# A recommendation kernel on Trainium2: history rows transposed into PSUM instead of through TensorE, and some rows fetched by SyncE

## The chip, the cores and the metric

The kernel runs on one core of a Trainium2 chip. The metric is the time of one execution on the device in microseconds; the median of three runs stands for a kernel. The core's engines are named as the profile names them: PE (TensorE, matrix products; PEld is its weight loading), DVE (VectorE), ACT (ScalarE), POOL (GpSimd) and SP (SyncE, which here only starts DMA transfers). PSUM is the memory into which PE writes; DVE and ACT can read and write it too. SBUF is the main memory on the core.

## The reference

A deep interest network for B = 16384 users with a history of L = 200 items each. Tables have D = 64 columns in float32, users and items 100000 rows.

```python
u, it, c = u_emb[user], i_emb[item], c_emb[cate]
h = i_emb[hist]                              # (200, 16384, 64)
itb = jnp.broadcast_to(it[None], h.shape)
feat = jnp.concatenate([h, itb, h - itb, h * itb], axis=-1)
a = dice(feat @ au_W1 + au_b1, au_alpha, axis=1)   # axis 1: over the users
w = a @ au_W2 + au_b2
cur = jnp.sum(w * h, axis=0)
z = jnp.concatenate([u, it, c, cur], axis=-1)
z = dice(z @ W1 + b1, alpha1, axis=0)
z = dice(z @ W2 + b2, alpha2, axis=0)
return z @ W3 + b3

def dice(x, alpha, axis):
    p = sigmoid((x - mean(x, axis)) * rsqrt(var(x, axis) + 1e-8))
    return x * (p + alpha * (1 - p))
```

Nearly all work is `h = i_emb[hist]`: 3.3 million rows of 256 bytes, each gathered from a random place, and the small attention layer on each. The mean and variance in `dice` go over all users of one history position, so no row of a position can be weighed before all its rows have been through the layer.

## The kernel before

The 16384 users are cut into 8 tiles of 2048 (128 partitions x 16 rows of 64). A step k handles tile c = k % 8 of history position l = k // 8; there are K = 1600 steps, in one list written out by hand (`step`), which each engine runs through in order. The engines are coupled by semaphores alone. In step k different things are done for different steps:

- SP starts `load_items(k + 1)` (L312): 512 KB of the transposed candidate items into one of four `itT` buffers. When c is 4 it also loads the indices of position l + 2 (L115).
- POOL does `fetch(k)`: 16 indirect gathers (L107), each 128 rows of 256 bytes, into one of 16 `rows` tiles.
- ACT does `gate(k - 10)` (L276): the sigmoid out of `xs` into PSUM buffer `pg`.
- `turn(k - 1)`: DVE transposes `rows` in 32x32 blocks into `hT` in SBUF, four instructions (L126); PE multiplies `hT` by the identity `same` into PSUM buffer `py` (through `layer`, L131), so that DVE can read the turned rows there.
- DVE adds the item's part (`hidden(k - 3)`, L300) and takes statistics (`measure(k - 3)`, two `bn_stats`, L305). When k - 3 is the last tile of a position, the norm follows: 28 small DVE instructions (L322 to L340, and the root in L142 to L148), and only then the gate.
- `product(k - 1)`: PE multiplies `hT` by `blk_h` into `px`; DVE forms `hm = py * itT` (L316); PE adds `hm` times `blk_m`.
- `weights(k - 10)` and `weigh(k - 10)` on DVE: L279 to L285 make the weights, L295 multiplies `rows` by them, L297 adds to `cur`.

A gather of step k may overwrite its `rows` tile when L295 of step k - 16, done in step k - 6, is through. So POOL can be up to six steps ahead of DVE, not more. Matrix products of float32 appear as two instructions each, so `layer` with one weight is four matmuls and four weight loads on PE.

Ahead of the loop the items are gathered and turned, the categories are looked up and the weights are laid out; after it come 128 gathers of user rows and the two upper layers.

Of the kernel before, what the change touches and what calls it, by code (L numbers as in the profile page):

```python
# [14 lines left out]
P = 128  # L15
D = 64
# [8 lines left out]
ITEMS = 4  # L25
IDX = 3


@with_exitstack
def din_kernel(  # L30
# [41 lines left out]
    def make(name, *shape, dt=F32):  # L72
        return const.tile(list(shape), dt, name=name)
# [18 lines left out]
    cur = [make(f"cur{c}", P, CD) for c in range(ND)]  # L92
    hm = make("hm", P, CD)
    total = py[:, :S]
    part = make("part", P, S)
    w = pg[:, :TD]
# [3 lines left out]
    ids = [idx[(i - 1) % IDX if i == 0 else (L + i - 1) % IDX] for i in range(2)]  # L100
    stats = [make(f"st{i}", P, 2 * ND, STATS) for i in range(3)]
    cate_ids = make("cate_ids", P, TD, dt=I32)
# [46 lines left out]

    same = make("same", P, P)  # L150
    blk_h = make("blk_h", P, P)
# [107 lines left out]
    def head_numbers():  # L259
# [3 lines left out]
        for t, n in ((same_a, ZA), (same_b, ZB)):  # L263
            nc.vector.tensor_single_scalar(lane, lanes, n - 1, ALU.bitwise_and)
            nc.vector.tensor_copy(t, lane)
            nc.vector.tensor_scalar(t, t, 0.0, n / P, ALU.is_equal, ALU.mult)

    def fetch(k):
# [9 lines left out]
    def weights(k):  # L278
        nc.vector.scalar_tensor_tensor(py, pg, au_1al, xs[k % XR], ALU.mult, ALU.mult)  # L279
        nc.vector.transpose(pg, py)  # L280
        nc.vector.reduce_sum(total, pg.rearrange("p (n a) -> p n a", a=S), axis=mybir.AxisListType.X)  # L281
        nc.vector.tensor_copy(part[P // 2 :], total[P // 2 :])  # L282
        for i in range(2):
            for g in range(2):
                nc.vector.scalar_tensor_tensor(  # L285
                    w[quarter(i, g)],
                    total[quarter(0, g), ts(i, TD)], au_bias2[quarter(0, g)], part[quarter(1, g), ts(i, TD)],
                    ALU.add, ALU.add,
                )

    def weigh(k):
        of = py.rearrange("p (n d) -> p n d", d=D)
        if k < ND:
            of = cur[k].rearrange("p (n d) -> p n d", d=D)
        nc.vector.tensor_mul(of, rows[k % ROWS], w.unsqueeze(2).to_broadcast([P, TD, D]))  # L295
        if k >= ND:
            nc.vector.tensor_add(cur[k % ND], py, cur[k % ND])  # L297

# [8 lines left out]
    def turn(k):  # L307
        transpose(hT[k % TURNED], rows[k % ROWS])
        layer(py, [(same, hT[k % TURNED])])

    def load_items(k):
        nc.sync.dma_start(itT[k % ITEMS], items[k % ND])  # L312

    def product(k):
        layer(px[k % 2], [(blk_h, hT[k % TURNED])], last=False)
        nc.vector.tensor_mul(hm, py, itT[k % ITEMS])  # L316
        layer(px[k % 2], [(blk_m, hm)], first=False)

# [25 lines left out]
    def step(k):  # L344

        def has(j):
            return 0 <= j < K

        if has(k + 1):
            load_items(k + 1)  # L350
        if has(k):
            l, c = divmod(k, ND)
            if c == 4 and l + 2 < L:
                load_hist_ids((l + 2) % IDX, l + 2)
            if c == 4 and l + 2 == L:
                load_ids(ids[1], r_user)
            fetch(k)
# [12 lines left out]
        if has(k - 1):  # L370
            product(k - 1)
        if has(k - LAG):
            weights(k - LAG)
            weigh(k - LAG)

    NK = -(-c_emb.shape[0] // P)
# [8 lines left out]
    def category_numbers():  # L385
# [22 lines left out]
        nc.vector.tensor_copy(of_row, rank)  # L408
        nc.vector.tensor_single_scalar(same, lanes, float(P), ALU.is_equal)

    def category(c, i):
# [17 lines left out]
        nc.scalar.copy(xs[c % XR][:, ts(i, CH)], to)  # L429

    with tc.manual_schedule():
        load_ids(ids[0], r_item)
        for l in range(min(2, L)):
            load_hist_ids(l, l)
        nc.sync.dma_start(cate_ids, r_cate.rearrange("(p n) -> p n", n=NT)[:, (ND - 1) * TD :])
        nc.gpsimd.iota(lanes, pattern=[[1, P]], base=P, channel_multiplier=-1)
# [3 lines left out]
        attention_weights()  # L440
        extra_unit()
        head_weights()

        halves_of = [(c, i) for c in range(ND - 1) for i in range(2)]
        for c in range(ND + 1):
# [13 lines left out]
            if c < ND:  # L459
                category(*halves_of.pop(0))  # L460
        load_items(0)
        head_numbers()
        for half in halves_of:
            category(*half)
        transpose(xs[ND - 1], rows[ND])
        for c in range(ND):
            nc.sync.dma_start(cates[c], xs[c % XR])

    za = [xs[(K - XR + c) % XR] for c in range(ND)]
# [183 lines left out]
```

## Time and profile before

| | |
|---|---|
| median of the runs | 38346.77 us |
| the runs | 38344.67, 38346.77, 38373.36 us |
| profiled execution | 38084.07 us |
| its span, first to last instruction | 38082.3 us |
| granted PE clock, mean | 0.646 |
| busy: PE / PEld | 14569.6 us (38%) / 5252.9 us (14%) |
| busy: DVE | 23384.9 us (61%) |
| busy: ACT | 2000.3 us (5%) |
| busy: POOL | 24410.9 us (64%) |
| DMA | 45 GB/s over the span |

The loop takes 98% of the span (its first product starts at 501.6 us, its last at 37813.6), and all its 40 slices on the page look alike, so one history position stands for the whole. No engine is busy for more than two thirds of the time. A row of a timeline gives start, duration, engine, line, operation and, in brackets, how long the engine had been idle and what ended it; "issue" is a wait for nothing that the profile shows, and "remote" one that something outside the record ended.

### The profile page before, as it was taken

Reading aid. Unit: us, or ns where it says so; the run is one execution under the profiler, and the core shown is the slowest. Engines: PE = TensorE matmul, PEld = TensorE weight load, DVE = VectorE, ACT = ScalarE, POOL = GpSimd, SP = SyncE. Lnnn points to the kernel's source line nnn. Section 1 sums busy time; section 2 is a strip of 40 time slices with the busy share of each in tenths; the row PEclk is TensorE's granted clock in tenths of the full one; section 3 lists DMA queues with packets and bytes.
Section 4 is the critical chain, followed back from the end, with each engine's and each line's share of the span. In section 5 each row is a group of like instructions: output and inputs, shape, how many; then the busy total and the mean of one; then the engine's idle time right before and its main releaser. Section 6 shows DMA issues by size and latency. Waiting matters only on the chain.

```text
span 38082.3 us, 118503 instructions
## 1 busy us (share of the span) xinstructions
PE 14569.6 (38%) x20100; PEld 5252.9 (14%) x20100; DVE 23384.9 (61%) x34932; ACT 2000.3 (5%) x1667; POOL 24410.9 (64%) x25879
## 2 busy tenths in 40 slices
PE   4333333333333333333333333333333333333334
PEld 1111111111111111111111111111111111111111
DVE  4666666666666666666666666666666666666666
ACT  0000000000000000000000000000000000000001
POOL 5666666666666666666666666666666666666665
PEclk7666666666666666666666666666666666666666
DMA  1111111111111111111111111111111111111111
GB/s 45 45 45 45 45 46 45 46 46 46 46 45 46 45 46 45 46 45 46 46 46 45 46 45 46 45 45 46 45 46 46 46 46 45 45 45 45 45 46 42
DMA packets 1103495, 1727.07 MB, mean 45 GB/s; under 512 B 454022, under 2 KB 479878, under 8 KB 1102726
## 3 DMA queue, kind: packets, MB, share of 16 engines
q0 software_dynamic: 827904, 849.43, 9.9%
q1 hardware_dynamic: 274246, 869.99, 6.7%
q14 instruction: 612, 5.01, 0.0%
q8 instruction: 157, 2.57, 0.0%
q10 hardware_dynamic: 576, 0.07, 0.0%
HBM read 1709.19 MB, written 8.52 MB: 45 GB/s over the span
## 4 chain that ended last, share of the span: by engine, by line
DVE 52%; another core or an unknown queue 26%; issue 14%; POOL 6%; DMA 1%; PE 1%; DVEq 1%; ACT 0%; POOLq 0%; ACTq 0%
DVE hT L126 10%; POOL rows L107 6%; DVE py L279 5%; DVE pg L280 5%; DVE hm L316 5%; DVE py L281 5%; DVE xs L300 4%; DVE py L295 4%; DVE pg L285 4%; DVE st L305 3%; DVE rs L148 1%; DVE t L147 1%; DVE t L146 1%; DMA rows<-in_L_rec_i_emb,idx 1%
## 5 line engine op out<-in xcount | busy, mean ns | idle before, releaser
L107 POOL DMA_INDIRECT rows<-in_L_rec_i_emb,idx x25728 | 24274.4, 944 | 13406.8 <-issue 7402.7
L131 PE MATMUL py<-hT,same 128*128 128x512 f32 x6400 | 6032.2, 1091 | 9968.1 <-DVE hT L126 5063.1
L131 PE MATMUL px<-hm,blk_m 128*128 128x512 f32 x6400 | 4506.7, 843 | 13260.1 <-DVE hm L316 7045.1
L316 DVE TENSOR_TENSOR hm<-py,itT 128x1024 f32<-128x1024 f32 x1600 | 1945.9, 1216 | 10239.3 <-remote 8060.6
L126 DVE STREAM_TRANSPOSE hT<-rows 64x512 f32<-64x512 f32 x6400 | 4499.9, 703 | 416.8 <-issue 327.6
L131 PE MATMUL px<-hT,blk_h 128*128 128x512 f32 x6400 | 3979.0, 755 | 1.0 <-issue 0.5
L276 ACT ACTIVATE pg<-xs,sh,rs 128x1024 f32<-128x1024 f32 x1600 | 1932.5, 1208 | 35232.2 <-DVE py L295 23733.1
L131 PEld LDWEIGHTS px<-hm,blk_m 128*128 128x128 f32 x6400 | 1530.6, 257 | 15673.8 <-DVE hm L316 7533.2
L131 PEld LDWEIGHTS py<-hT,same 128*128 128x128 f32 x6400 | 1771.9, 311 | 13673.5 <-DVE hT L126 7103.9
L279 DVE SCALAR_TENSOR_TENSOR py<-pg,au_1al,xs 128x1024 f32<-128x1024 f32 x1600 | 2068.3, 1293 | 540.1 <-remote 213.3
L131 PEld LDWEIGHTS px<-hT,blk_h 128*128 128x128 f32 x6400 | 1787.4, 282 | 2881.9 <-issue 2339.1
L280 DVE STREAM_TRANSPOSE pg<-py 128x1024 f32<-128x1024 f32 x1600 | 2024.5, 1265 | 172.3 <-DVE py L279 122.2
L305 DVE BATCH_NORM_STATS2 st<-xs 128x6 f32<-128x512 f32 x3200 | 2058.4, 685 | 55.0
L300 DVE TENSOR_TENSOR xs<-px,itp 128x1024 f32<-128x1024 f32 x1600 | 1959.7, 1225 | 130.0 <-issue 83.4
L281 DVE TENSOR_REDUCE py<-pg 128x32 f32<-128x1024 f32 x1600 | 1972.7, 1233 | 72.5 <-DVE pg L280 0.8
L295 DVE TENSOR_TENSOR py<-rows,pg 128x1024 f32<-128x1024 f32 x1592 | 1957.3, 1229 | 55.3 <-issue 0.7
L297 DVE TENSOR_TENSOR cur<-py,cur 128x1024 f32<-128x1024 f32 x1592 | 1948.5, 1224 | 56.3 <-issue 0.9
L285 DVE SCALAR_TENSOR_TENSOR pg<-py,au_bias,part 32x16 f32<-32x16 f32 x6400 | 1530.6, 239 | 227.6 <-issue 1.2
L147 DVE SCALAR_TENSOR_TENSOR t<-t,v 128x1 f32<-128x1 f32 x808 | 131.0, 162 | 608.2 <-DVE t L146 268.1
L148 DVE SCALAR_TENSOR_TENSOR rs<-t,rs 128x1 f32<-128x1 f32 x800 | 129.2, 161 | 605.5 <-DVE t L147 396.5
L146 DVE TENSOR_TENSOR t<-rs 128x1 f32<-128x1 f32 x800 | 127.8, 160 | 468.6 <-DVE rs L148 262.0
L282 DVE COPY part<-py 64x32 f32<-64x32 f32 x1600 | 311.2, 195 | 88.0 <-DVE py L281 32.0
(158 smaller groups left out, 1835.2 us busy)
## 6 DMA issues: line engine op xcount, KB each, us to landing
itT<-items SPq DMA_DIRECT2D x1608, 512.0 KB
rows<-in_L_rec_i_emb,idx POOLq DMA_INDIRECT x25728
idx<-in_r_hist SPq DMA_DIRECT2D x200, 64.0 KB
items<-itT SPq DMA_DIRECT2D x8, 512.0 KB
cates<-xs SPq DMA_DIRECT2D x8, 512.0 KB
itp<-cates SPq DMA_DIRECT2D x8, 512.0 KB
rows<-in_L_rec_u_emb,idx POOLq DMA_INDIRECT x128
cur<-in_L_rec_c_emb SPq DMA_DIRECT2D x14, 32.0 KB
```

Of the source, the lines that this page charges most:

```text
L107: nc.gpsimd.indirect_dma_start(out=dst[:, n, :], out_offset=None, in_=table, in_offset=bass.IndirectOffsetOnAxis(ap=ids, axis=0),)
L126: nc.vector.transpose(by_tile(dst[ts(e, D)], i)[:, n0:n1], of[ts(i, D), n0:n1, ts(e, S)])
L131: nc.tensor.matmul(dst[:, ts(i, CH)], lhsT, rhs[:, ts(i, CH)], start=(first and j == 0), stop=(last and j == len(pairs) - 1), skip_group_c ...
L279: nc.vector.scalar_tensor_tensor(py, pg, au_1al, xs[k % XR], ALU.mult, ALU.mult)
L280: nc.vector.transpose(pg, py)
L281: nc.vector.reduce_sum(total, pg.rearrange("p (n a) -> p n a", a=S), axis=mybir.AxisListType.X)
L285: nc.vector.scalar_tensor_tensor(w[quarter(i, g)], total[quarter(0, g), ts(i, TD)], au_bias2[quarter(0, g)], part[quarter(1, g), ts(i, TD) ...
L295: nc.vector.tensor_mul(of, rows[k % ROWS], w.unsqueeze(2).to_broadcast([P, TD, D]))
L297: nc.vector.tensor_add(cur[k % ND], py, cur[k % ND])
L300: nc.vector.tensor_add(xs[k % XR], px[k % 2], itp[k % ND])
L305: nc.vector.bn_stats(stats[l % 3][:, 2 * c + i, :], xs[k % XR][:, ts(i, CH)])
L316: nc.vector.tensor_mul(hm, py, itT[k % ITEMS])
```

## The change

The turned rows are written by DVE straight into PSUM, as the four transposes now have `py` as destination. The identity product is gone. ACT copies `py` to `hT` in SBUF for PE, and DVE multiplies `py` by `itT` in `turn` itself, right behind the transposes, into one of two `hms`. `product` is then one PE group of `blk_m` times `hms` and `blk_h` times `hT`. In `weights` and `weigh` the buffers `pg` and `py` change roles. `load_items` runs one step further ahead.

In every second l, the last of the 16 row groups of tile c = 7 isn't gathered by POOL: SP loads a list of its 128 indices, DVE multiplies them by 256 (the bytes of a row), SP loads them 32 at a time into registers and starts 128 DMAs of one row each, eight per step, into a buffer of its own; when all have landed ACT copies the buffer into the `rows` tile (`place`). So 100 gathers of 25600 go.

```diff
+PERIOD = 2
+BY_SP = ((1, 7),)
+GROUP = 32
+AHEAD = 1
...
-    same = make("same", P, P)
...
+    def load_list(l):
...
+                nc.sync.dma_start(of[:, s : s + 1], v[:, c : c + 1])
...
+            nc.vector.tensor_scalar_mul(list_of(l), list_of(l), ROW)
...
+        def pump(self, upto):
+            while self.done < upto:
+                m, r = divmod(self.done, P)
+                if r % GROUP == 0:
...
+                    _, self.at = nc.values_load_multi_w_load_instructions(
+                        list_of(p * PERIOD + l)[:, j : j + GROUP],
...
+                row = flat[ds(self.at[r % GROUP], ROW)].rearrange("(o d) -> o d", o=1)
+                dst = self.slots[m % SLOTS].bitcast(U8)[r : r + 1]
+                dma = self.queue.dma_start(dst, row).then_inc(self.landed[m % SLOTS], 16)
...
+        def take(self, m):
+            fence = self.queue.wait_ge(self.landed[m % SLOTS], 16 * P)
...
     def fetch(k):
         l, c = divmod(k, ND)
-        for n in range(TD):
+        for n in range(TD - (side(k) is not None)):
...
+    def place(k, taken):
+        if taken is not None:
+            nc.scalar.copy(rows[k % ROWS][:, TD - 1], taken)
...
     def weights(k):
-        nc.vector.scalar_tensor_tensor(py, pg, au_1al, xs[k % XR], ALU.mult, ALU.mult)
-        nc.vector.transpose(pg, py)
-        nc.vector.reduce_sum(total, pg.rearrange("p (n a) -> p n a", a=S), axis=mybir.AxisListType.X)
+        nc.vector.scalar_tensor_tensor(pg, pg, au_1al, xs[k % XR], ALU.mult, ALU.mult)
+        nc.vector.transpose(py, pg)
+        nc.vector.reduce_sum(total, py.rearrange("p (n a) -> p n a", a=S), axis=mybir.AxisListType.X)
...
     def turn(k):
-        transpose(hT[k % TURNED], rows[k % ROWS])
-        layer(py, [(same, hT[k % TURNED])])
+        transpose(py, rows[k % ROWS])
+        nc.scalar.copy(hT[k % TURNED], py)
+        nc.vector.tensor_mul(hms[k % TURNED], py, itT[k % ITEMS])
...
     def product(k):
-        layer(px[k % 2], [(blk_h, hT[k % TURNED])], last=False)
-        nc.vector.tensor_mul(hm, py, itT[k % ITEMS])
-        layer(px[k % 2], [(blk_m, hm)], first=False)
+        layer(px[k % 2], [(blk_m, hms[k % TURNED]), (blk_h, hT[k % TURNED])])
...
-        if has(k + 1):
-            load_items(k + 1)
+        if has(k + 2):
+            load_items(k + 2)
...
             fetch(k)
+            q, m = side(k) or (None, None)
+            taken = q and q.take(m)
+        by_sync.pump(by_sync.until(k + 1))
...
         if has(k - LAG) and not norm:
             gate(k - LAG)
+        if has(k):
+            place(k, taken)
```

One step on DVE, from the transposes of one step to the sum into `cur`, before, with what each instruction waits for (the numbers behind names are buffers; DMAHW and DMASW are transfers, PE, DVE and Activation the engines):

```order
L316 TENSOR_TENSOR hm<-py,itT_98 128x1024 [waits DMAHW3_49,PE_49]
L279 SCALAR_TENSOR_TENSOR py<-pg,au_1al,xs_93 128x1024 [waits DVE_49,Activation_49]
L280 STREAM_TRANSPOSE pg<-py 128x1024 [waits DVE_49]
L281 TENSOR_REDUCE py<-pg 128x32 [waits DVE_49]
L282 COPY part<-py 64x32 [waits DVE_49]
L285 SCALAR_TENSOR_TENSOR pg<-py,au_bias_154,part 32x16 [waits DVE_49] x4
L295 TENSOR_TENSOR py<-rows_75,pg 128x1024 [waits DVE_49]
L297 TENSOR_TENSOR cur_121<-py,cur_121 128x1024 [waits DVE_49]
L126 STREAM_TRANSPOSE hT_87<-rows_85 64x512 [waits DMASW4_49,DMASW5_49,DMASW3_49,DMASW6_49,DMASW2_49,DMASW7_49,DMASW1_49,DMASW0_49]
L126 STREAM_TRANSPOSE hT_87<-rows_85 64x512 x3
L300 TENSOR_TENSOR xs_93<-px_67,itp_131 128x1024
L305 BN_STATS st_137<-xs_93 128x6 [waits DVE_49]
```

and now:

```order
L137 STREAM_TRANSPOSE py<-rows_82 64x512 [waits DMASW4_49,DMASW5_49,DMASW3_49,DMASW6_49,DMASW2_49,DMASW7_49,DMASW1_49,DMASW0_49]
L137 STREAM_TRANSPOSE py<-rows_82 64x512 [waits DVE_49] x3
L397 TENSOR_TENSOR hm_124<-py,itT_96 128x1024 [waits DMAHW3_49,Activation_49]
L387 TENSOR_TENSOR xs_90<-px_66,itp_129 128x1024 [waits PE_49]
L392 BN_STATS st_139<-xs_90 128x6 [waits DVE_49]
L392 BN_STATS st_139<-xs_90 128x6
L366 SCALAR_TENSOR_TENSOR pg<-pg,au_1al,xs_91 128x1024
L367 STREAM_TRANSPOSE py<-pg 128x1024 [waits DVE_49]
L368 TENSOR_REDUCE pg<-py 128x32 [waits DVE_49]
L369 COPY part<-pg 64x32 [waits DVE_49]
L372 SCALAR_TENSOR_TENSOR py<-pg,au_bias_155,part 32x16 [waits DVE_49] x4
L382 TENSOR_TENSOR pg<-rows_73,py 128x1024 [waits DVE_49]
```

The product with `itT` has moved from behind the statistics to right behind the transposes, and it waits for Activation (the copy of `py` by ACT) where it waited for PE. The number of DVE instructions in a step is the same, 18.

Two steps on PE before (each row is one half of the columns or both; two recorded instructions and two weight loads stand behind each matmul):

```order
L131 MATMUL py<-hT_87,same 128x512 x2
L131 MATMUL px_67<-hT_87,blk_h 128x512 x2
L131 MATMUL px_67<-hm,blk_m 128x512 x2
L131 MATMUL py<-hT_86,same 128x512 x2
L131 MATMUL px_66<-hT_86,blk_h 128x512 x2
L131 MATMUL px_66<-hm,blk_m 128x512 x2
```

and now:

```order
L142 MATMUL px_66<-hm_124,blk_m 128x512 [waits DVE_49]
L142 MATMUL px_66<-hT_86,blk_h 128x512 [waits Activation_49]
L142 MATMUL px_66<-hm_124,blk_m 128x512
L142 MATMUL px_66<-hT_86,blk_h 128x512
L142 MATMUL px_67<-hm_125,blk_m 128x512 [waits DVE_49]
L142 MATMUL px_67<-hT_87,blk_h 128x512 [waits Activation_49]
```

Six matmuls of a step have become four, and PE now waits for ACT's copy too.

SP before had one row a step, and the indices once in eight:

```order
L312 DMA itT_96<-items_104 128x1024
L312 DMA itT_97<-items_105 128x1024
L115 DMA idx_135<-in_r_hist 128x128
L312 DMA itT_98<-items_106 128x1024
```

and now, where the buffer of a tile is taken and the next one begun:

```order
L400 DMA itT_97<-items_105 128x1024 [waits DMAHW2_49,DVE_49]
L338 ISA [waits sp_landed2]
L323 TENSOR_LOAD lists [waits DMAHW0_49,DVE_49]
L330 DMA sp_rows_176<-in_L_rec_i_emb 1x256 [waits Activation_49]
L330 DMA sp_rows_176<-in_L_rec_i_emb 1x256 x7
L400 DMA itT_98<-items_102 128x1024 [waits DMAHW3_49,DMAHW0_49,DVE_49]
L330 DMA sp_rows_176<-in_L_rec_i_emb 1x256 x8
```

SP has nine DMAs a step where it had one, the wait for the landed rows (L338) stands among them, and all of `itT` queues behind it.

More of the change, by code (lines that the diff above doesn't have):

```diff
@@ L92, in din_kernel @@
     cur = [make(f"cur{c}", P, CD) for c in range(ND)]
-    hm = make("hm", P, CD)
-    total = py[:, :S]
+    hms = [make(f"hm{i}", P, CD) for i in range(TURNED)]
+    hm = hms[0]
+    total = pg[:, :S]
     part = make("part", P, S)
-    w = pg[:, :TD]
+    w = py[:, :TD]
     itp = [make(f"itp{c}", P, CD) for c in range(ND)]
@@ L429, in category, with before @@
         nc.scalar.copy(xs[c % XR][:, ts(i, CH)], to)
+    def before(k):
+        for q in queues:
+            q.pump(q.until(k + 1))
     with tc.manual_schedule():
@@ L441, in din_kernel @@
         extra_unit()
+        for l in range(min(2, L)):
+            scale_list(l)
         head_weights()
```

68 lines of the change are left out of this document (63 added, 5 removed).

## The prediction

> **What bounds the kernel now.** I read the waits first, then the rows of single lines, the table by stretches and the timelines. Columns of the waits: total us, times, longest.
>
> ```profile
> span 38082.3 us, 118503 instructions
> POOL rows L107 <- issue: 7444.5, 24418, 0.6
> POOL rows L107 <- DVE py L295: 5534.8, 592, 13.0
> DVE hm L316 <- remote: 8060.6, 478, 27.0
> L316 DVE TENSOR_TENSOR hm<-py,itT x1600: 1205/1224/1226, 501.6 to 37813.6; 128x1024 f32<-128x1024 f32 x178
> ```
>
> The 1600 steps run from 501.6 to 37813.6 us, 23.34 us a step, 186.7 us for the eight steps of one history position (an l). POOL waits for VectorE's L295, which frees a `rows` tile, and VectorE waits long at L316, where the name "remote" says that no recorded work ended the wait. The stretches show that nothing in the loop is busy all the time:
>
> ```profile
> core 0: us, PE busy (x) PEld busy (x) DVE busy (x) ACT busy (x) POOL busy (x), PEclk, DMA share, GB/s
> 19017.18:19203.30 186.12, 71.25 (x96) 26.02 (x96) 115.37 (x173) 9.60 (x9) 120.74 (x128) 0.65 0.17 46
> 499.30:658.90 159.60, 50.87 (x92) 19.93 (x92) 42.65 (x53) 0.19 (x1) 120.80 (x128) 0.67 0.20 56
> 19045.50:19059.80 14.30, 7.59 (x12) 2.94 (x12) 13.76 (x19) 1.21 (x1) 10.64 (x13) 0.75 0.21 62
> 19080.70:19114.30 33.60, 10.39 (x12) 3.65 (x12) 13.86 (x19) 1.21 (x1) 25.47 (x27) 0.55 0.16 42
> ```
>
> One l has 128 gathers, 192 PE instructions (96 matmuls, 96 weight loads) and 173 DVE instructions. Unhindered, POOL issues 128 gathers in 159.6 us, far below 186.7. One and the same step takes 14.30 us in one place and 33.60 in another. 33.60 is 24 PE instructions times 1.40 us. The same 1.40 stands between the instructions of other engines, in other work:
>
> ```profile
> 689.09 0.16 DVE L148 SCALAR_TENSOR_TENSOR rs<-t,rs 128x1 f32<-128x1 f32 x1
> 689.28 0.16 DVE L146 TENSOR_TENSOR t<-rs 128x1 f32<-128x1 f32 x1
> 19179.08 0.16 DVE L147 SCALAR_TENSOR_TENSOR t<-t,v 128x1 f32<-128x1 f32 x1 [0.21 <-issue]
> 19180.48 0.16 DVE L148 SCALAR_TENSOR_TENSOR rs<-t,rs 128x1 f32<-128x1 f32 x1 [1.24 <-issue]
> 19181.88 0.16 DVE L146 TENSOR_TENSOR t<-rs 128x1 f32<-128x1 f32 x1 [1.24 <-issue]
> 16.11 1.86 SPq L181 DMA_DIRECT2D rows<-in_L_rec_au_W  x4
> 96.33 0.71 SPq L256 DMA_DIRECT2D alb<-in_L_rec_alpha  x1
> 97.73 0.71 SPq L255 DMA_DIRECT2D w2b<-in_L_rec_W  x1
> ```
>
> VectorE's tiny norm operations follow each other after 0.19 us when free and after 1.40 when braked; SyncE's DMAs take 0.47 each early and come 1.40 apart later. So some outlet lets each engine finish one instruction per 1.40 us, each engine on its own account, whatever the instruction is. When does the brake end?
>
> ```profile
> 499.32 0.94 POOL L107 DMA_INDIRECT rows<-in_L_rec_i_emb,idx  x1 [106.80 <-DVE xs L126]
> 657.89 0.94 POOL L107 DMA_INDIRECT rows<-in_L_rec_i_emb,idx  x1 [0.30 <-issue]
> 666.68 1.22 DVE L316 TENSOR_TENSOR hm<-py,itT 128x1024 f32<-128x1024 f32 x1 [25.61 <-remote]
> 678.70 1.23 DVE L316 TENSOR_TENSOR hm<-py,itT 128x1024 f32<-128x1024 f32 x1 [5.42 <-remote]
> 690.91 1.22 DVE L316 TENSOR_TENSOR hm<-py,itT 128x1024 f32<-128x1024 f32 x1
> 700.33 0.94 POOL L107 DMA_INDIRECT rows<-in_L_rec_i_emb,idx  x1 [41.49 <-DVE cur L295]
> ```
>
> POOL issues 128 gathers from 499.32 to 657.89 and stops. The braked steps go on for 20 us with POOL idle, and end at 678.70: 499.32 + 128 x 1.40 = 678.52. From there everything runs at its own speed (next product 12.2 us later) until POOL starts again. So a gather, issued every 1.25 us, runs up a debt of 1.40, and while the debt is open every engine is braked. An engine isn't braked at once; it has a reserve, which fills only as far as it is faster than the outlet, and is empty again when the debt is paid.
>
> This gives one l as **128 x 1.40 = 179.2 us plus the time in which POOL owes nothing and waits**, 186.8 - 179.2 = 7.6 us. (186.8 is the steady mean: 1590 steps from 690.91 to 37813.6.) PE needs 192 instructions, the outlet passes 128 in 179.2 us, the other 64 come from PE's reserve, filled more than once in an l. PE is what holds VectorE's L316, that holds the weighing at L295, and that holds POOL.
>
> [...]
>
> **The change, part by part.**
>
> *Removed on PE.*
>
> ```profile
> L131 PE MATMUL py<-hT,same 128*128 128x512 f32 x6400 | 6032.2, 1091 | 9968.1 <-DVE hT L126 5063.1
> L131 PEld LDWEIGHTS py<-hT,same 128*128 128x128 f32 x6400 | 1771.9, 311 | 13673.5 <-DVE hT L126 7103.9
> ```
>
> 6400/1600 = 4 matmuls and 4 loads a step go: 24 PE instructions become 16, 128 in an l, 22.4 us a step if always braked. 128 x 1.40 = 179.2 us, the length of POOL's own debt, so PE stops holding anything.
>
> *Removed on POOL.* 16 of 128 gathers lose one in every second l: 0.5 of 128. The debt of an l becomes 127.5 x 1.40 = **178.5 us**, the floor under any l in which POOL is not idle. Worth 0.7 us.
>
> *VectorE.* A step keeps 18 instructions: 4 transposes, `hms`, hidden, two `bn_stats`, and 10 of the weighing. In the order of the change (shown above) L397 waits for ScalarE's copy of the same `py`.
>
> ```profile
> 690.84 0.16 DVE L340 TENSOR_TENSOR sh<-sh,open 128x1 f32<-128x1 f32 x1
> 692.37 1.21 ACT L276 ACTIVATE pg<-xs,sh,rs 128x1024 f32<-128x1024 f32 x1
> 693.61 1.29 DVE L279 SCALAR_TENSOR_TENSOR py<-pg,au_1al,xs 128x1024 f32<-128x1024 f32 x1 [1.47 <-ACT pg L276]
> 698.83 1.22 DVE L295 TENSOR_TENSOR cur<-rows,pg 128x1024 f32<-128x1024 f32 x1
> L126 DVE STREAM_TRANSPOSE hT<-rows 64x512 f32<-64x512 f32 x6400 | 4499.9, 703 | 416.8 <-issue 327.6
> L280 DVE STREAM_TRANSPOSE pg<-py 128x1024 f32<-128x1024 f32 x1600 | 2024.5, 1265 | 172.3 <-DVE py L279 122.2
> ```
>
> The copy isn't in the trace of before; ScalarE's sigmoid over the same 128x1024 out of the same kind of operands takes 1.21, so I take 1.21 plus two handovers of some 0.12, 1.45 us a step (bounds: 1.2 if the handovers overlap, 2.0). A free step grows from 14.30 to 15.75. Cover: POOL spends 20 us on a tile (16 gathers, 158.57/127 = 1.25 apart from 499.32 to 657.89), so 15.75 stays under it; without that cover the copy would cost 8 x 1.45 = 11.6 us an l. A transpose into PSUM costs no more than into SBUF: L280 writes PSUM with 1265 ns for 1024 columns, L126 SBUF with 703 for 512. The rewritten weights swap `pg` and `py` between the same operations: 0.
>
> *The new braked engine.* With PE out of the way VectorE is the engine with the most instructions: 8 x 18 + 28 of the norm + half a list scaling = 172.5 an l. Its reserve comes from this stretch:
>
> ```profile
> 19154.48 0.94 POOL L107 DMA_INDIRECT rows<-in_L_rec_i_emb,idx  x1 [12.54 <-DVE py L295]
> 19154.48:19179.08 24.60, 13.66 (x20) 5.26 (x20) 23.23 (x44) 0.97 (x1) 18.81 (x20) 0.72 0.18 47
> ```
>
> POOL's debt begins at 19154.48; VectorE gets 44 instructions through before its first braked one at 19179.08, while the outlet passes 24.60/1.40 = 17.6: a reserve of about 26 (bounds 22, and 32, PE's 64 spread over two fillings).
>
> Now I lay one l of the new kernel out, from POOL's restart after the weighing of the norm step (t = 0). Free steps end at 15.75, 31.5 and 47.25. A free step runs 18 in 15.75 us, of which 11.25 pass, so 6.75 go to the reserve: it is full after 26/6.75 = 3.9 steps, at 61 us. From there a step takes 18 x 1.40 = 25.2: ends at about 64, 89, 114, 140. POOL, 20 us a tile, is held by none of these for more than a microsecond, has issued its eight tiles at 160, and is held by the norm step, which has 46 instructions. Debt paid at 178.5. By then VectorE has done 26 + 178.5/1.40 = 153.5 of 172.5; 19 are left before POOL is free: 10 of the norm (10 x 0.19 = 1.9 us), the gate (1.21 and handovers, 1.45), L366 to L382 (693.61 to 698.83 + 1.22 = 6.44), and 0.28 to POOL's start (700.05 to 700.33). Together **10.1 us**, in which POOL owes nothing. One l is 178.5 + 10.1 = **188.6 us**, against 186.8. POOL waits once an l instead of several times, but longer, since the step that frees it is the one with the norm and the gate in it.
>
> *SyncE.* 8 one-row DMAs and one of `itT` a step: 9 x 1.40 = 12.6 us of 23.6 (bounds: 9 x 0.47 = 4.2; two passages for each row, 8 x 2.8 + 1.4 = 23.8, a rival). *ScalarE's* copy of 128x64 in every 16th step has a sixteenth of the sigmoid's elements: below 1.21, while POOL is on the tile; hidden.
>
> *Sum.* +1.8 us x 199 l = +358 us on the profiled 38084 (span 38082.3): 38442. The timed median lies 263 above the profiled execution; I carry that over: **38700 us**. With a reserve of 32 there are 13 left, 3 of the norm: 8.8 us, 187.3; if the gate also runs ahead, 186.9. With 22, 14 of the norm: 10.9, 189.4. The likeliest case's own range is 38370 to 38870.
>
> **The rivals.**
>
> *PE slow by its own clock.* Then the third that is removed sets the time free. Granted clock 0.55 in the slow step and 0.75 in the fast one speak for it; against it, 1.36 in clock doesn't make 33.60 from 14.30, and VectorE and SyncE keep the same 1.40. The loop would be POOL's: 159.6 x 127.5/128 = 159.0, so 38347 - 200 x 27.8 = 32790; if steps only shrink to 22.4 us, 36830. [...]
>
> *Several short waits an l.* If POOL's debt reaches zero twice in some l, VectorE's reserve is filled twice (52 + 127.5 > 172.5), it is never braked, and only short waits remain: 183 to 185, at 184 **37790**. For it: the old kernel does this. Against: a tile adds only 16 x 0.15 = 2.4 us of debt beyond POOL's own time, but by the sixth tile that is 14.4 us, and POOL would have to wait that long at a step that is 5 us longer than its tile.
>
> *SyncE becomes the bound.* If a row addressed by a register passes twice, 23.8 us a step, 190.4 an l, **39070**. It decides from (23.6 - 1.4)/8 = 2.8 us a row. Against: a DMA passes once in the rows of L255 and L256.
>
> *The change does nothing measurable.* The two effects cancel (reserve above 30): 186.4 to 187.2.
>
> **How the numbers follow.** The runs shown of this kernel differ by 0.1%, so 0.2% (77 us, 0.38 us an l) can be told from no change. Forecast, above 187.2: 0.48. SyncE or a longer norm wait, above 190: 0.05. No change: 0.14. Several waits: 0.27. PE's clock: 0.06. So slower 0.53, same 0.14, faster 0.33. The range goes from 36800 (the several-waits case, and the 22.4-us steps) to 39100 (SyncE); some 0.1 lies below, 0.07 above.
>
> **What would show it.** Right: no 33.6-us steps; VectorE steps of about 25.2 us, its norm operations 1.40 apart; one POOL wait an l, of 28 us, ended by the norm step's L382; l near 188.6. Wrong: several POOL waits an l, or VectorE never braked (then 178.5 to 186), or a gather cadence that fills the loop (159 an l).

## The result and the profile after

| | before | after |
|---|---|---|
| median of the runs | 38345.72 us | 38641.13 us |
| lowest, highest | 38339.95, 38373.36 | 38635.07, 38646.9 |
| span of the profiled execution | 38082.3 us | 38633.2 us |
| busy: PE / DVE | 14569.6 / 23384.9 us | 9969.7 / 23473.6 us |
| busy: ACT / POOL | 2000.3 / 24410.9 us | 3635.5 / 24314.7 us |

The changed kernel is slower: 1.0077 of the time before, 95% interval 1.0061 to 1.0093. TensorE has lost a third of its instructions, POOL a little, and the kernel has gained nothing from either. By the profiled executions the distance is larger, 551 us against 295; the one profiled before was 0.7% shorter than its own runs, the one after is as long as its runs. No trace of a longer execution of before exists, so that difference stays open; the mechanism is read from the traces, the size from the runs.

The waits of the changed kernel (total us, times, longest, chosen rows):

```profile
POOL rows L118 <- issue: 7761.6, 24670, 5.6
POOL rows L118 <- DVE pg L382: 5956.6, 648, 26.3
DVE py L372 <- issue: 4248.9, 3667, 1.9
DVE hm L397 <- issue: 1048.0, 838, 15.9
DVE hm L397 <- ACT hT L396: 881.8, 762, 1.4
```

and the rows of that product's line:

```profile
L397 DVE TENSOR_TENSOR hm<-py,itT x1600: 1224/1224/1227, 509.1 to 38364.7; 128x1024 f32<-128x1024 f32 x178
```

From this line, one l is (38364.7 - 509.1)/1599 x 8 = 189.4 us. The 10218 us for which VectorE stood before its product with `itT` (8060.6 + 2157.1) are 1930 now. In their place stands the wait for nothing before L372, the four small additions of a step, 3667 times and never longer than 1.9 us: the 1.40 us of the outlet has moved from TensorE to VectorE. VectorE's first use of TensorE's result, at L387, has no idle time before it in the whole trace (busy us, mean ns, idle time before it):

```profile
L387 DVE TENSOR_TENSOR xs<-px,itp 128x1024 f32<-128x1024 f32 x1600 | 1943.4, 1215 | 0.0
```

Of POOL's waits in one l the timeline has these:

```profile
19097.99 0.94 POOL L118 DMA_INDIRECT rows<-in_L_rec_i_emb,idx  x1 [18.65 <-DVE pg L382]
19198.94 0.94 POOL L118 DMA_INDIRECT rows<-in_L_rec_i_emb,idx  x1 [1.39 <-issue]
19224.28 0.94 POOL L118 DMA_INDIRECT rows<-in_L_rec_i_emb,idx  x1 [5.64 <-DVE pg L382]
19249.48 0.94 POOL L118 DMA_INDIRECT rows<-in_L_rec_i_emb,idx  x1 [5.55 <-DVE pg L382]
19287.08 0.94 POOL L118 DMA_INDIRECT rows<-in_L_rec_i_emb,idx  x1 [19.18 <-DVE pg L382]
```

From restart to restart, 19097.99 to 19287.08, are 189.09 us, with 127 gathers. Their debt is 127 x 1.40 = 177.8 us and is paid at 19275.8; added up gather by gather, it stays above zero through the three shorter waits. Some of VectorE's rows before and around that moment:

```profile
19240.98 0.20 DVE L369 COPY part<-pg 64x32 f32<-64x32 f32 x1 [0.34 <-issue]
19242.38 0.23 DVE L372 SCALAR_TENSOR_TENSOR py<-pg,au_bias,part 32x16 f32<-32x16 f32 x1 [1.20 <-issue]
19243.78 0.24 DVE L372 SCALAR_TENSOR_TENSOR py<-pg,au_bias,part 32x16 f32<-32x16 f32 x1 [1.17 <-issue]
19264.79 0.16 DVE L412 COPY other<-mv 32x2 f32<-32x2 f32 x1 [1.24 <-issue]
19266.19 0.16 DVE L412 COPY other<-mv 32x2 f32<-32x2 f32 x1 [1.24 <-issue]
19274.61 0.15 DVE L153 TENSOR_SCALAR v<-var 128x1 f32<-128x1 f32 x1 [1.17 <-DVE var L422]
19275.31 0.15 DVE L154 TENSOR_SCALAR t<-v 128x1 int32<-128x1 int32 x1 [0.55 <-DVE v L153]
19276.02 0.15 DVE L155 TENSOR_SCALAR rs<-t 128x1 int32<-128x1 int32 x1 [0.56 <-DVE t L154]
19276.21 0.16 DVE L157 TENSOR_TENSOR t<-rs 128x1 f32<-128x1 f32 x1
19276.40 0.16 DVE L158 SCALAR_TENSOR_TENSOR t<-t,v 128x1 f32<-128x1 f32 x1
19278.93 0.16 DVE L426 TENSOR_TENSOR sh<-sh,open 128x1 f32<-128x1 f32 x1
19280.36 1.29 DVE L366 SCALAR_TENSOR_TENSOR pg<-pg,au_1al,xs 128x1024 f32<-128x1024 f32 x1 [1.28 <-ACT pg L363]
19285.58 1.23 DVE L382 TENSOR_TENSOR pg<-rows,py 128x1024 f32<-128x1024 f32 x1
```

Up to 19274.61 most of the norm's small instructions start 1.40 us after the one before; two then take 0.70, and from 19276.02 on, 0.2 us after the debt is paid by that sum, they follow each other after 0.19. What was left of the norm (16 instructions), the gate and the weighing take until 19286.81, POOL starts at 19287.08, and the time without debt is 11.3 us. By stretches:

```profile
core 0: us, PE busy (x) PEld busy (x) DVE busy (x) ACT busy (x) POOL busy (x), PEclk, DMA share, GB/s
19097.99:19275.79 177.80, 45.42 (x64) 17.68 (x64) 106.74 (x147) 16.55 (x15) 119.84 (x127) 0.62 0.20 48
19148.30:19173.60 25.30, 5.79 (x8) 2.23 (x8) 13.27 (x18) 2.22 (x2) 19.20 (x21) 0.63 0.21 48
```

A braked step takes 25.3 us for its 18 VectorE instructions. While the debt was open, VectorE got 147 instructions through, 20 more than the outlet's 127: its reserve.

### The profile page after: what moved, and what is told of

It is laid out like the page before. It is cut to its first block, busy times and chain, and to the rows that moved or that the text cites. A ratio compares the mean times of both kernels' runs of the same rounds, so it can differ in the third digit from the quotient of the medians.

```text
span 38633.2 us, 133929 instructions
## 1 busy us (share of the span) xinstructions
PE 9969.7 (26%) x13700; PEld 3829.1 (10%) x13700; DVE 23473.6 (61%) x35031; ACT 3635.5 (9%) x3367; POOL 24314.7 (63%) x25779
## 4 chain that ended last, share of the span: by engine, by line
DVE 45%; issue 36%; POOL 13%; ACT 2%; another core or an unknown queue 2%; DMA 1%; PE 1%; DVEq 0%; SPq 0%; ACTq 0%; POOLq 0%
POOL rows L118 13%; DVE py L137 9%; DVE pg L366 4%; DVE st L392 4%; DVE py L367 4%; DVE pg L368 4%; DVE hm L397 4%; DVE pg L382 4%; DVE xs L387 4%; DVE py L372 3%; ACT hT L396 1%; DMA rows<-in_L_rec_i_emb,idx 1%; ACT pg L363 1%; DVE part L369 1%
## 5 line engine op out<-in xcount | busy, mean ns | idle before, releaser
L142 PE MATMUL px<-hm,blk_m 128*128 128x512 f32 x6400 | 5692.7, 988 | 28377.3 <-DVE xs L387 21202.1
L137 DVE STREAM_TRANSPOSE py<-rows 64x512 f32<-64x512 f32 x6400 | 4617.6, 721 | 3037.5 <-issue 1762.1
L142 PE MATMUL px<-hT,blk_h 128*128 128x512 f32 x6400 | 4724.5, 831 | 0.0
L372 DVE SCALAR_TENSOR_TENSOR py<-pg,au_bias,part 32x16 f32<-32x16 f32 x6400 | 1527.6, 239 | 4382.5 <-issue 4248.9
L382 DVE TENSOR_TENSOR pg<-rows,py 128x1024 f32<-128x1024 f32 x1592 | 1957.0, 1229 | 1154.9 <-issue 1123.7
L366 DVE SCALAR_TENSOR_TENSOR pg<-pg,au_1al,xs 128x1024 f32<-128x1024 f32 x1600 | 2068.8, 1293 | 861.7 <-issue 596.1
L396 ACT COPY hT<-py 128x1024 f32<-128x1024 f32 x1600 | 1619.2, 1012 | 9788.2 <-DVE py L137 8747.2
L384 DVE TENSOR_TENSOR cur<-pg,cur 128x1024 f32<-128x1024 f32 x1592 | 1949.2, 1224 | 207.7 <-DVE pg L382 90.0
L367 DVE STREAM_TRANSPOSE py<-pg 128x1024 f32<-128x1024 f32 x1600 | 2025.2, 1266 | 54.5
L368 DVE TENSOR_REDUCE pg<-py 128x32 f32<-128x1024 f32 x1600 | 1972.8, 1233 | 54.4
L387 DVE TENSOR_TENSOR xs<-px,itp 128x1024 f32<-128x1024 f32 x1600 | 1943.4, 1215 | 0.0
```

Source lines behind the costliest of these rows:

```text
L137: nc.vector.transpose(by_tile(dst[ts(e, D)], i)[:, n0:n1], of[ts(i, D), n0:n1, ts(e, S)])
L142: nc.tensor.matmul(dst[:, ts(i, CH)], lhsT, rhs[:, ts(i, CH)], start=(first and j == 0), stop=(last and j == len(pairs) - 1), skip_group_c ...
L366: nc.vector.scalar_tensor_tensor(pg, pg, au_1al, xs[k % XR], ALU.mult, ALU.mult)
L367: nc.vector.transpose(py, pg)
L368: nc.vector.reduce_sum(total, py.rearrange("p (n a) -> p n a", a=S), axis=mybir.AxisListType.X)
L372: nc.vector.scalar_tensor_tensor(w[quarter(i, g)], total[quarter(0, g), ts(i, TD)], au_bias2[quarter(0, g)], part[quarter(1, g), ts(i, TD) ...
```

## The experiments

The groups of runs each had runs of the kernel before beside them, and these took 37937, 38047 and 38080 us. So runs of different groups are compared by their ratio to before, runs of one group also directly. In the table, "l" comes from the first and the last product with `itT` in each trace, the debt is the number of gathers in an l times 1.40 us, and the rest is what remains: the time in which POOL owes nothing. The changed kernel itself stands there twice, 1.0077 and 1.0110 in two groups, where `after_again` was expected to repeat the first; so 0.3% between runs of different groups is no effect.

| run | ratio to before, 95% | l | debt | rest |
|---|---|---|---|---|
| before (first profile) | 1 | 186.7 | 179.2 | 7.5 |
| after (first profile) | 1.0077 (1.0061 to 1.0093) | 189.4 | 178.5 | 10.9 |
| merge | 0.9963 (0.9949 to 0.9977) | 185.2 | 178.5 | 6.7 |
| split | 1.0106 (1.0089 to 1.0122) | 187.8 | 178.5 | 9.3 |
| swap | 1.0109 (1.0092 to 1.0126) | 188.0 | 178.5 | 9.5 |
| half | 0.7113 (0.7099 to 0.7128) | 131.1 | 89.6 | 41.5 |
| after_again | 1.0110 (1.0094 to 1.0127) | 188.5 | 178.5 | 10.0 |
| psum_only | 1.0091 (1.0074 to 1.0108) | 188.2 | 179.2 | 9.0 |
| sp_only | 1.0051 (1.0034 to 1.0068) | 187.5 | 178.5 | 9.0 |
| lean | 0.9709 (0.9670 to 0.9748) | 180.9 | 178.5 | 2.4 |
| less_pe | 1.0038 (1.0024 to 1.0052) | 187.3 | 179.2 | 8.1 |
| merge_before | 0.9909 (0.9892 to 0.9925) | 184.9 | 179.2 | 5.7 |
| rows_double | 1.0757 (1.0735 to 1.0778) | 201.1 | 177.8 | 23.3 |
| lean_no_rows | 0.9796 (0.9780 to 0.9812) | 182.8 | 179.2 | 3.6 |

### Is the brake POOL's debt? Half of the gathers

```diff
-        for n in range(TD - (side(k) is not None)):
+        for n in range(0, TD, 1 if k < ROWS else 2):
```

> The changed kernel with every second gather left out after the first 16 steps (the odd row groups of a tile keep old rows, so the output is not the reference's); everything else as it was. Theory of the debt: 8 gathers owe 11.2 us, less than a free step of 15.75, so the debt is paid in every step, no engine is braked, and l is VectorE's own time, 8 x 15.75 + 5.6 of the norm + 2.8 for the gate = 134 us: about 27600 us. Rival (the 1.40 us is a property of the engines or of their clock, not of POOL's debt): steps stay at 25 us, l at 189 or more, 38600.

Measured: 26985 us, 131.1 us per l. One l as a stretch, and two products with `itT` in the timeline, one step apart:

```profile
core 0: us, PE busy (x) PEld busy (x) DVE busy (x) ACT busy (x) POOL busy (x), PEclk, DMA share, GB/s
19021.90:19153.10 131.20, 48.23 (x64) 18.43 (x64) 116.04 (x174) 17.92 (x17) 60.53 (x64) 0.66 0.18 49
```

```profile
19104.66 1.23 DVE L397 TENSOR_TENSOR hm<-py,itT 128x1024 f32<-128x1024 f32 x1 [1.16 <-ACT hT L396]
19120.12 1.23 DVE L397 TENSOR_TENSOR hm<-py,itT 128x1024 f32<-128x1024 f32 x1 [1.16 <-ACT hT L396]
```

TensorE's and VectorE's work is that of the changed kernel, instruction for instruction (64 and 64, 174), the granted clock is 0.66 against 0.62, and a step without the norm takes 15.46 us. VectorE is busy for 116 of 131 us, and the norm's small instructions, 1.40 us apart in after, follow each other after 0.20:

```profile
19142.83 0.16 DVE L157 TENSOR_TENSOR t<-rs 128x1 f32<-128x1 f32 x1
19143.03 0.16 DVE L158 SCALAR_TENSOR_TENSOR t<-t,v 128x1 f32<-128x1 f32 x1
```

So the 25 and 33 us of a braked step are no property of these engines; they come with the gathers, and vanish where 8 of them owe 11.2 us in a step of 15.5. The rival falls.

### Is it TensorE's number of instructions that bounds the kernel before? A product left out

```diff
-        layer(px[k % 2], [(blk_h, hT[k % TURNED])], last=False)
         nc.vector.tensor_mul(hm, py, itT[k % ITEMS])
-        layer(px[k % 2], [(blk_m, hm)], first=False)
+        layer(px[k % 2], [(blk_m, hm)])
```

> The kernel before with the product of hT and blk_h left out (its output is not the reference's): 64 TensorE instructions fewer per l, 128 instead of 192, as many as the changed kernel has; VectorE's order, buffers and waits as before, no copy by ScalarE, no rows by SyncE. Theory of the outlet: TensorE is out, VectorE with 173 instructions per l and a reserve of 27 takes over, one time without debt per l, 179.2 + 9.9 = 189 us: 1.010 of before, slower although work was removed. Rival (TensorE's own speed bounds the kernel before): faster, 0.96 (steps of 22.4 us) to 0.86 (POOL's 159.6 us per l).

Measured: 1.0038, no faster, though a third of TensorE's instructions was gone and nothing was added. The stretch from a restart of POOL on, for the 179.2 us of the debt, and the rows of the product's line:

```profile
core 0: us, PE busy (x) PEld busy (x) DVE busy (x) ACT busy (x) POOL busy (x), PEclk, DMA share, GB/s
19076.27:19255.47 179.20, 53.07 (x60) 15.24 (x60) 106.87 (x159) 8.22 (x7) 120.85 (x128) 0.59 0.18 44
```

```profile
L315 DVE TENSOR_TENSOR hm<-py,itT x1600: 1203/1207/1226, 505.1 to 37945.2; 128x1024 f32<-128x1024 f32 x178
```

VectorE gets 159 through where the outlet passes 128: here its reserve is 31, larger than the 27 on which the expectation rested, so the rest is 8.1 instead of 9.9 us and the loss smaller than expected. A loss of 0.4% is hardly more than what two groups differ by; what tells the theories apart is that there is no gain: with TensorE's own speed as the bound this run would have been at least 4% faster, by the expectation's estimate from steps of 22.4 us.

### VectorE's instructions, fewer and more

`merge` (after) and `merge_before` (before) do the four weight additions of a step as two:

```diff
         for i in range(2):
-            for g in range(2):
-                nc.vector.scalar_tensor_tensor(
-                    w[quarter(i, g)],
-                    total[quarter(0, g), ts(i, TD)], au_bias2[quarter(0, g)], part[quarter(1, g), ts(i, TD)],
-                    ALU.add, ALU.add,
-                )
+            nc.vector.scalar_tensor_tensor(
+                w[ts(i, D)],
+                total[:D, ts(i, TD)], au_bias2[:D], part[D:, ts(i, TD)],
+                ALU.add, ALU.add,
+            )
```

> The changed kernel with the four 32-partition weight additions of a step done as two of 64 partitions: 16 VectorE instructions fewer per l, some 4 us less VectorE work per l. Theory (each engine passes one instruction per 1.40 us while POOL's gathers are owed, reserve of VectorE 18 as the trace of after shows): at the end of the debt 8.5 instructions instead of 24.5 are left, POOL's wait without debt falls from 11 us to 7.9, l from 189.4 to 186.3, so about 38000 us. Rival (POOL's own rate sets the l): no change, 38640.

> The kernel before with the weight additions merged as in the run merge: 16 VectorE instructions fewer per l. Theory: TensorE's 192 instructions set the time here, so only the 0.5 us by which the weighing is shorter counts, in each of the two times without debt of an l: 0.995 of before (0.99 to 1.0). Rival (VectorE's instructions bound this kernel too): 0.985 or less.

`split` cuts two instructions of a step of after into halves:

```diff
-        nc.vector.tensor_mul(of, rows[k % ROWS], w.unsqueeze(2).to_broadcast([P, TD, D]))
+        for i in range(2):
+            n = ts(i, TD // 2)
+            nc.vector.tensor_mul(of[:, n], rows[k % ROWS][:, n], w[:, n].unsqueeze(2).to_broadcast([P, TD // 2, D]))
         if k >= ND:
-            nc.vector.tensor_add(cur[k % ND], pg, cur[k % ND])
+            for i in range(2):
+                nc.vector.tensor_add(cur[k % ND][:, ts(i, CH)], pg[:, ts(i, CH)], cur[k % ND][:, ts(i, CH)])
```

> The changed kernel with the two last VectorE instructions of a step (rows times weights, sum into cur) cut into halves: 16 VectorE instructions more per l, work the same but for some 0.06 us a cut, 1 us per l. Theory of the outlet: 40.5 instructions are left when the debt is paid, the whole norm runs free after it, 15.5 us of wait instead of 11, l about 194, 39500 us. Rival (VectorE's time counts, not its number of instructions): at most +1 us per l, 38640 to 38840.

Measured against before: merge 0.9963, and after 1.0077 or 1.0110 in the two groups that had it; so the merging is worth 1.1 to 1.5% of the changed kernel, and 1.4% against `swap` (next section), which is as slow as the changed kernel and ran in the group of merge. The expected 1.7% (38000 of 38641) is a little more than that. In merge POOL's only wait of an l ends at

```profile
19057.98 0.95 POOL L118 DMA_INDIRECT rows<-in_L_rec_i_emb,idx  x1 [26.52 <-DVE pg L381]
19243.10 0.94 POOL L118 DMA_INDIRECT rows<-in_L_rec_i_emb,idx  x1 [26.60 <-DVE pg L381]
```

185.12 us apart, 7.3 us beyond 127 x 1.40: between these two gathers the layout of the prediction, with one wait per l, is what the trace has.

merge_before gained 0.9%, more than the 0.5% expected, at the edge of its range, and less than the rival's 1.5%. The two times without debt of an l became 0.81 and 0.95 us shorter (means of 191 l: 3.05 to 2.24 and 4.68 to 3.73), not only the 0.5 by which the weighing is shorter. So VectorE's instructions may count in the kernel before too: the prediction's rows at 19179 to 19182 have its norm braked to 1.40 us, and the weighing that frees POOL comes behind it. That this makes up the remaining 0.3 to 0.45 us wasn't shown.

split was 1.0106 where the outlet's theory wanted 2.2% above after (39500 against 38641). By its time alone it is what the rival expected, by which VectorE's time counts and not its number of instructions. The single steps decide against that rival. From one product with `itT` to the next, in a braked step of merge and in one of split:

```profile
19127.46 1.23 DVE L396 TENSOR_TENSOR hm<-py,itT 128x1024 f32<-128x1024 f32 x1 [1.16 <-issue]
19149.87 1.23 DVE L396 TENSOR_TENSOR hm<-py,itT 128x1024 f32<-128x1024 f32 x1 [1.16 <-ACT hT L395]
```

```profile
18980.28 1.22 DVE L400 TENSOR_TENSOR hm<-py,itT 128x1024 f32<-128x1024 f32 x1 [1.16 <-ACT hT L399]
19008.28 1.23 DVE L400 TENSOR_TENSOR hm<-py,itT 128x1024 f32<-128x1024 f32 x1 [1.16 <-issue]
```

These are 22.41 and 28.00 us, 16 x 1.40 = 22.4 and 20 x 1.40 = 28.0, where after has 25.2; a free step, with the same instructions, takes 14.9 us in merge, 15.7 in split and 15.5 in after. So the cuts do lengthen a braked step by what the outlet wants. POOL's waits in split show why that did not lengthen the l:

```profile
19024.87 0.95 POOL L118 DMA_INDIRECT rows<-in_L_rec_i_emb,idx  x1 [2.94 <-DVE pg L384]
19052.86 0.95 POOL L118 DMA_INDIRECT rows<-in_L_rec_i_emb,idx  x1 [8.29 <-DVE pg L384]
19074.81 0.95 POOL L118 DMA_INDIRECT rows<-in_L_rec_i_emb,idx  x1 [2.23 <-DVE pg L384]
19100.02 0.95 POOL L118 DMA_INDIRECT rows<-in_L_rec_i_emb,idx  x1 [5.50 <-DVE pg L384]
19127.02 0.95 POOL L118 DMA_INDIRECT rows<-in_L_rec_i_emb,idx  x1 [8.53 <-DVE pg L384]
```

POOL waits in nearly every step, and some of these waits fall where little is owed. Adding up 1.40 us per gather over its trace, the debt comes to zero 338 times in 200 l (305 times with 1.402 us, as in some waits almost nothing is owed), where after has 200 by both, so by the theory VectorE's reserve can fill more often. That is the pattern of the prediction's second rival, and with it the loss by longer steps did not appear in the time: split is as slow as `swap` in the same group (38332 and 38351 us).

### ScalarE's copy

```diff
         transpose(py, rows[k % ROWS])
-        nc.scalar.copy(hT[k % TURNED], py)
         nc.vector.tensor_mul(hms[k % TURNED], py, itT[k % ITEMS])
+        nc.scalar.copy(hT[k % TURNED], py)
```

> The changed kernel with the two readers of py in the other order: VectorE multiplies by itT right behind its transposes, ScalarE copies after that. VectorE no longer waits for the copy, some 1.2 us a step less when it runs free. Theory of the outlet: the number of instructions is the same, so l stays at 189.4 and the time at 38640 within 100. Rival (the wait for ScalarE's copy is what made the change slower): 8 x 1.2 us per l less, 36700; if it counts in the three free steps of an l alone, 37900.

Measured: 1.0109, as slow as the changed kernel in the group that had it again (1.0110) and not faster than in the first (1.0077). VectorE no longer waits for the copy (in the whole trace it stood 374 us before its product with `itT`, L396 there, where after has the 1930), and the time did not follow. The rival is out. The absolute time (38351) is below the expectation's only because before was faster in that group too.

### The two parts alone

`psum_only` is after without a tile for SyncE (`BY_SP = ()`); `sp_only` is before with SyncE's rows added and everything of `turn`, `product`, `weights` and `weigh` as it was. `after_again` is the changed kernel beside them.

> The changed kernel once more, to stand on the same chip as the others of this group. 1.0077 of the time before; in its trace one time without debt per l, 11.3 us long, VectorE 19 instructions beyond what the outlet passes.

> The changed kernel without SyncE's rows: POOL gathers all 128 per l again, the transposes still go to PSUM. Theory of the outlet: the debt of an l grows from 178.5 to 179.2 us, E stays at 11, so 0.35% slower than the changed kernel, 1.011 of before. Rival (SyncE's 64 row transfers of an l with their register loads hold up itT or fill the outlet): faster than the changed kernel, 1.004 of before or less.

> The kernel before with SyncE's rows alone: TensorE still passes the turned rows on, 192 of its instructions per l. Theory of the outlet: the debt shrinks by 0.7 us, two times without debt per l as before: 0.996 of before. Rival (SyncE's rows cost time): 1.004 or more.

Both expectations on SyncE were wrong; sp_only came out as its rival had it. The PSUM part alone costs 0.9%. SyncE's rows cost 0.5% by themselves and 0.2% on top of the PSUM part (38465 against 38394 us in the same group, spreads of 22 and 16), although they take half a gather off each l; the two don't add up. The debt falls by 0.7 us as it should, and the rest grows by 1.0 (on top of the PSUM part) or 1.5 us (by themselves, against the first profile of before). After's own trace shows what the prediction had taken too cheaply, in the line's instructions (count, duration min/median/max in ns) and in the timeline of SyncE's queue:

```profile
L330 SPq MOVE sp_rows<-in_L_rec_i_emb x12800: 1/698/1437, 377.5 to 38329.0; - x197
L330 SPq DMA_DIRECT2D sp_rows<-in_L_rec_i_emb x12800: 1/699/1423, 377.5 to 38330.4; - x197
```

```profile
19105.41 7.87 SPq L330 DMA_DIRECT2D sp_rows<-in_L_rec_i_emb  x8
19120.20 18.34 SPq L330 DMA_DIRECT2D sp_rows<-in_L_rec_i_emb  x8
```

Each row is a register move and a transfer, and both carry the 0.70 us; from 19122.44 on, a move, a transfer (19123.84) and the next move (19125.24) start 1.40 us apart. The second eight rows take 18.34 us, though the first of them still ran free, and not 8 x 1.40 = 11.2.

On top of the PSUM part, the loss can be found in what VectorE gets through. Two stretches, each from a restart of POOL on for the length of its debt, first after_again, then psum_only (columns as above):

```profile
19012.91:19190.71 177.80, 47.95 (x64) 18.50 (x64) 107.41 (x152) 16.55 (x15) 119.83 (x127) 0.61 0.19 48
19343.50:19522.70 179.20, 45.40 (x64) 17.65 (x64) 108.14 (x157) 16.55 (x15) 120.77 (x128) 0.63 0.20 47
```

VectorE's instructions beyond the outlet's, its reserve, are 25 in the first and 29 in the second. Counted so over 194 l of each trace, the mean is 20.0 in after, 23.8 in after_again, 26.6 in swap, 28.1 in psum_only and 31.6 in less_pe, and the time without debt falls in the same order: 11.3, 10.5, 9.9, 9.4 and 8.5 us. But after and after_again, the same kernel, already differ by 3.8; so that SyncE's rows lower this number fits, and isn't shown.

### How near SyncE is to being the bound

```diff
-BY_SP = ((1, 7),)
+BY_SP = ((0, 7), (1, 7))
```

> The changed kernel with the last row group of tile 7 fetched by SyncE in every l, not in every second: 16 rows a step, SyncE's instructions per l from 152 to about 284 (a register move and a transfer for each row). Theory (each of the two passes the outlet): 127 + 25 pass while the debt of 177.8 us is open, some 130 are left at 0.2 to 0.3 us each: 205 us per l, 1.09 of before. Rival (a row passes once): SyncE needs 148, nothing changes but half a gather: 1.007 of before.

Measured: 1.0757, l 201.1, between the two and nearer the theory. POOL waits twice in an l, 16.7 and 26.7 us, where after had one wait of 19 us and shorter ones; by the sum of its gathers, the debt is paid in both:

```profile
19027.13 0.95 POOL L118 DMA_INDIRECT rows<-in_L_rec_i_emb,idx  x1 [16.71 <-DVE pg L382]
19153.42 0.94 POOL L118 DMA_INDIRECT rows<-in_L_rec_i_emb,idx  x1 [26.71 <-DVE pg L382]
19228.45 0.94 POOL L118 DMA_INDIRECT rows<-in_L_rec_i_emb,idx  x1 [16.67 <-DVE pg L382]
```

What now ends late is SyncE's work: the copy of its rows by ScalarE (L359) waits for it in nearly every l.

```profile
ACT rows L359 <- SPq L336: 7060.4, 197, 59.5
```

So a row passes twice, and at 16 rows a step SyncE is the bound. In after the same copy has no idle time before it, and only six of 1600 products with `itT` waited longer than 2.1 us, as many as in psum_only; so neither late rows nor late `itT` loads are what eight rows a step cost. Why VectorE would get fewer instructions through with them stays open.

### A version that beats both

`lean` is after with the merged additions, the order of `swap`, three Newton steps of the root in place of four, and the norm's pairing of partition halves (four copies, a sum, two halvings) as one TensorE product with a fixed matrix:

```diff
+        both = pg[:, :2]
+        nc.tensor.matmul(both, pair, mv, start=True, stop=True)
...
-        nc.vector.tensor_sub(dev, mv[:, 0:1], mean)
+        nc.vector.tensor_sub(dev, mv[:, 0:1], both[:, 0:1])
...
-        for _ in range(4):
+        for _ in range(3):
```

> The changed kernel with fewer VectorE instructions: two weight additions instead of four a step, three Newton steps instead of four in the root, the pairing of the norm's halves (four copies, a sum, two halvings) done by one small TensorE product, and the product with itT ahead of ScalarE's copy. 146.5 VectorE instructions per l instead of 172.5, fewer than the 127.5 + 26 that outlet and reserve pass while the debt is open. Theory: E falls from 11 us to about 1, l to 179.5 to 181, 0.965 of before (0.96 to 0.975). Rival (after VectorE, SyncE with its 150 instructions or the gate behind the norm sets the end): 0.98 to 0.99.

> The run lean without SyncE's rows: 128 gathers per l, debt 179.2 us, no SyncE work but itT and indices. Theory: 0.7 us more debt, a larger reserve of VectorE (28 as in psum_only): 0.970 of before within 0.004, as lean. Rival (SyncE's rows take part of the reserve, and in lean hold the end): 0.965 or less.

lean takes 36961 us (its four runs 36762 to 37085), 0.971 of before (0.967 to 0.975) and 0.961 of the changed kernel in the same group (36961/38465). Its l is 180.9 us, 2.4 above the debt: VectorE has 146.5 instructions in an l, about as many as the 127.5 of the debt and a reserve of 20, and what is left is POOL's 127.5 x 1.40. By the sum of the gathers the debt comes to zero only 144 times in its 200 l, and 101 times without SyncE's rows: in the other l POOL is still owing when it goes on. The rows of SyncE, which cost in the changed kernel, don't cost here: without them (lean_no_rows) it is 0.980, where 0.970 was expected and the rival had 0.965; the debt is 0.7 us longer and the rest 1.2. Why the rest is longer without SyncE's rows is open.

## Why the prediction was right

The forecast was 38700 us, 0.9% above before; measured were 38641, 0.8%.

- **TensorE stops holding anything.** Shown: VectorE never stands before L387, and `less_pe`, which takes away the same number of TensorE instructions and nothing else, is no faster by itself.
- **VectorE becomes the braked engine, 25.2 us a step.** Shown: 25.2 us is the commonest step, its small instructions 1.40 apart, and two instructions fewer or more make it 22.4 or 28.0.
- **The floor, 178.5 us of debt per l, and the end of the brake.** Shown: the norm's instructions go from 1.40 to 0.19 us apart at 19276.02, the sum gives 19275.8. `half` shows that the brake goes with the debt.
- **The time without debt, 10.1 us.** It was 11.3 in the l shown, and 10.9 and 10.0 in the table for the two profiled executions. The reserve had been put at 26; it was 20 in the first trace. With 20, 25 are left, 16 of the norm (3.0 us), and 1.45 + 6.44 + 0.28 more: 11.2. So the form of the term was right, and the reserve in it too large for this kernel. The reserve is not one number: 20 and 24 in the two traces of after, 22 in `merge`, 28 in `psum_only`, 32 in `less_pe`. (With a reserve of 32, 4 instructions of the norm are left and not 3: 8.9 us for the prediction's 8.8.)
- **One wait of 28 us.** Not so in after: 19 us, and about 13 us in shorter ones, since the braked steps, each 5 us longer than POOL's tile, began to hold POOL earlier than laid out. "Several POOL waits an l" was on the prediction's own list of what would show it wrong, and this part of the layout was wrong. But the several-waits rival needs a debt that reaches zero twice, and in after it does so once (200 times in 200 l); the sum over an l does not depend on how POOL's waits are divided. In `merge` it came out as one wait of 26.5.
- **ScalarE's copy is hidden.** Its price was 1.01 us (the mean of L396 in after) and not 1.21, a free step 15.46 (in `half`) and not 15.75, and `swap` shows that taking the wait away changes nothing that could be measured.
- **SyncE's rows are hidden and take 0.7 us off.** This step was wrong. A row passes the outlet twice, as the SyncE rival had it, though without its price: the rows cost 0.2 to 0.5% where -0.35% had been put down. The 1.0 us that they add to the rest on top of the PSUM part is about what the reserve's term was off, and may be the same thing: without them, in `psum_only`, the reserve is 28 and the rest 9.0.
- **Carrying over the 263 us** between the profiled execution and the median. It did not hold: the profiled execution after is 8 us below its median. By the profiled executions alone the forecast was 38442 against 38633, 191 us or 1.0 us an l too low, about what the reserve's term was off; the offset happened to make up for it. That the end figure agrees to 0.2% is in part luck.

## What to carry to other kernels

Look for a spacing that is the same on several engines and for unlike instructions; then count instructions before microseconds, and cut those of the engine that has the most, small ones included. (`split` is the warning: more instructions made its braked steps longer, 28.0 us for 25.2, and the time the same, while POOL's debt ran out 338 times where after has 200.) While such an outlet binds, an instruction of 0.2 us costs as much as one of 1.2 (in after the 0.23 us of L372 at 19242.38 and the 1.23 us of L382 at 19247.98 each stood 1.40 us before the next), and work moved from one engine to another one gained nothing here, where the other was the next in number. Take the bound away first by the smallest edit (here: two additions merged, then the norm's small ones), and let each edit run by itself: of the two parts of this change neither was the gain that its own sum of work had promised.

## What the runs showed of the hardware

While POOL's gathers are owed, 1.40 us each where POOL issues one per 1.25, VectorE passes one instruction per 1.40 us once a reserve is used up, 20 instructions in after and 32 in `less_pe`; TensorE's 24 instructions of a braked step of before took 33.60 us, 24 x 1.40, and in after a register move of SyncE counts like a transfer (medians 698 and 699 ns at L330). A third fewer TensorE instructions did not make the kernel before faster (`less_pe`, 1.0038). In the trace of before the debt comes to zero 403 times in 200 l, in that of `less_pe` 201 times: TensorE's larger number went with two times without debt in each l. Whether each of them also refilled VectorE's reserve was not measured. What the outlet is, and why it passes one instruction per 1.40 us, no run here showed.
